# Group norm and attention on one core: the block sums moved into the accumulator's PSUM bank, the side work of the bursts reordered, the last two blocks inverted on VectorE

## Chip, cores and metric

One core of one Trainium2 chip. The metric is the time of one execution in device microseconds. Engines are named as in the profile: PE (TensorE matmul), PEld (weight load), DVE (VectorE), ACT (ScalarE), POOL (GpSimd), SP (the queue that issues DMA).

## The reference

```python
# x: (4, 512, 48, 48) fp32, so T = 2304 tokens per image, 8 heads of 64 channels
hn  = group_norm(x, 32 groups)
qkv = qkv_w @ hn + qkv_b                      # to fp16
w   = softmax((q * s).T @ (k * s))            # per image and head, 2304 x 2304
a   = w @ v                                   # fp32
out = x + proj_w @ a + proj_b
```

## The kernel before

The 16 pairs of heads (4 per image) are worked through in blocks of 512 queries (the last of each pair has 256). A block is 6 **bursts** (3 for the short one). A burst is three tiles of scores on PE, three exponentials on ACT, and the values of the burst before. There are 432 bursts, 108 per image ("batch"). Beside them runs a **list** of other PE work, cut into pieces: q, k and v chains of the coming pairs, and the output projection of the image before. A rule (`fill`) hands out pieces burst by burst.

The softmax's denominators: DVE adds the bursts' exponentials of a block into one tile (`acc`), and PE then sums that tile over its partitions with a matrix of ones (`sl`). PSUM has eight banks: three score tiles of two banks each, one bank for the accumulated values (`av`), one for all list chains (`pw`).

Names in the profile: `ps` are scores, `p` exponentials, `avx` and `slx` the copies of `av` and `sl` out of PSUM, `pqk` and `pv` the chains of q, k and v, `pr` the projection, `r` a residual tile (input and then output of a projection chain), `att` an attention result and `a` its conversion for the projection, `gmean` the group means of the next image's norm.

```python
    def values(u):
        ...
        if k == 0:
            av[0] = ps_av.tile([P, QB], F32, tag="av", ...)      # the only such bank
        ...                                                      # 6 or 12 matmuls
        if last:
            nc.vector.tensor_copy(avx[g, j][:, :n], av[0][:, :n])

    def add(u):
        ...
        nc.vector.tensor_tensor(acc[g, j], before, pt, ALU.add)

    def add_up(g, j):
        sl = chain_bank(f"sl_{g}_{j}")                           # the list's bank
        ...                                                      # matmuls: ones16 x acc
        nc.vector.tensor_copy(sx[:, :n], sl[:, :n])
        ...                                                      # the rows go out by DMA

    for n in range(len(stream) + 4):                             # one turn per burst
        scores(stream[n])
        values(stream[n - 1])
        add(stream[n - 1])
        if ended(n - 3):
            divide(*stream[n - 3][:2])      # inverses: to DRAM, back as rows, times avx
        if ended(n - 2):
            add_up(*stream[n - 2][:2])      # sums, and no list work in this burst
        else:
            fill(n, ended(n - 1))           # list work; closes the open chain at a block's end
    # cut: tails and conditions
```

A chain is four pieces of 4 matmuls (q, k, v), or one piece of 8 (projection).

## Time and profile before

| | before |
|---|---|
| median | 1800.25 us (4 runs, 1797.93 to 1801.34) |
| span of the profiled run | 1796.6 us |
| start to the first score | 120.5 us |
| batches of 108 bursts, by the starts of their first scores | 413.1, 435.5, 433.2 us |
| last batch, to the first score of its last burst | 353.3 us |
| from there to the end (tail) | 41.0 us |

The batch rows are read from the start times of the score matmuls. The lines of the profile stand in the prediction.

### The profile page before, as it was taken

To read this page: it belongs to the slowest core of one execution; us is meant where nothing else is said; L and a number is where in the kernel's file an instruction comes from. 1 tells how busy PE (TensorE), PEld (TensorE's weight loads), DVE (VectorE), ACT (ScalarE), POOL (GpSimd) and SP (SyncE) were. 2 spreads that over 40 slices of the span, in tenths; PEclk is the share of its full clock that TensorE was granted. 3 is DMA by queue.
4 is the path that set the end of the run, shared out by engine and by line. 5 is a ranking of instruction groups with operands and counts; after the bars stand their busy time and mean duration, and the time that the engine had idled before them with its cause. 6 is when DMAs were issued, how large, how long until landed. Compare 5 with 4: busy or idle time off the path is not lost. (4 is left out here: it accounts for less than half of the span.)

```text
span 1796.6 us, 26704 instructions
## 1 busy us (share of the span) xinstructions
PE 1652.7 (92%) x10706; PEld 649.1 (36%) x10706; DVE 1030.8 (57%) x1194; ACT 1220.1 (68%) x1297; POOL 334.7 (19%) x561
## 2 busy tenths in 40 slices
PE   4999997999999989899999998989999999999885
PEld 1333332333333343433333344343333334334443
DVE  5226557656555555756455555675555566666663
ACT  0027776677787775866677777685667888887971
POOL 1000122111121123210011113231011111222331
PEclk9999999999999999999999999999999999999998
DMA  5001022000000043310000014330000001104233
GB/s 194 0 1 31 19 50 78 10 13 13 10 14 16 17 112 118 90 39 13 10 13 16 13 40 122 107 92 13 13 10 13 14 15 23 53 16 132 61 107 110
DMA packets 90406, 82.15 MB, mean 46 GB/s; under 512 B 51488, under 2 KB 58144, under 8 KB 90272
## 3 DMA queue, kind: packets, MB, share of 16 engines
q1 hardware_dynamic: 83712, 62.75, 12.9%
q0 software_dynamic: 4592, 14.18, 2.7%
q10 hardware_dynamic: 1968, 3.41, 0.6%
q8 instruction: 86, 1.41, 0.3%
q14 instruction: 48, 0.39, 0.1%
HBM read 60.83 MB, written 19.17 MB: 45 GB/s over the span
## 5 line engine op out<-in xcount | busy, mean ns | idle before, releaser
L803 ACT ACTIVATE p<-ps 128x1024 f16<-128x1024 f32 x1296 | 1218.8, 1038 | 523.6 <-PE ps L796 523.4
L655 PE MATMUL pqk<-x,wqkv 128*64 128x512 f32 (+1 forms) x2560 | 530.4, 551 | 6.4 <-DVE x L628 4.4
L853 DVE TENSOR_TENSOR acc<-acc,p 128x3072 f16<-128x3072 f16 x272 | 482.3, 1773 | 31.0 <-ACT p L803 29.5
L796 PE MATMUL ps<-q,k 64*128 64x512 f16 (+1 forms) x2880 | 388.2, 360 | 64.0 <-ACT p L803 63.1
L820 PE MATMUL av<-p,v 128*64 128x512 f16 (+1 forms) x2880 | 363.7, 366 | 0.6 <-DVE avx L829 0.6
L655 PEld LDWEIGHTS pqk<-x,wqkv 128*64 128x64 f32 x2560 | 179.4, 137 | 255.3 <-issue 196.7
L796 PEld LDWEIGHTS <-k 64*128 64x128 f16 x2880 | 119.3, 94 | 412.3 <-issue 366.9
L696 PE MATMUL pv<-wqkv,x 128*64 128x512 f32 x1152 | 260.7, 599 | 4.3 <-DVE x L628 4.3
L885 POOL TENSOR_SCALAR in<-sums 128x8 f32<-128x8 f32 (+1 forms) x160 | 55.1, 345 | 964.3 <-DMA sums<-slx 957.9
L820 PEld LDWEIGHTS <-v 128*64 128x64 f16 x2880 | 125.6, 109 | 188.9 <-issue 149.6
L898 POOL TENSOR_TENSOR att<-avx,ib 128x512 f16<-128x512 f32 (+1 forms) x70 | 105.6, 1508 | 303.4 <-DMA ib<-row 275.9
L853 DVE TENSOR_TENSOR acc<-p,p 128x3072 f16<-128x3072 f16 x80 | 145.1, 1814 | 24.8 <-ACT p L803 24.7
L735 PE MATMUL pr<-a,whi 128*128 128x512 f32 (+1 forms) x320 | 126.1, 401 | 19.2 <-DVE r L743 10.3
L706 DVE TENSOR_TENSOR v<-pv,bv 128x256 f16<-128x256 f32 x144 | 54.4, 420 | 144.1 <-PE pv L696 144.0
L696 PEld LDWEIGHTS pv<-wqkv,x 128*64 128x64 f32 x1152 | 81.3, 138 | 148.2 <-issue 131.3
L664 DVE TENSOR_SCALAR k<-pqk,bqkv 128x512 f16<-128x512 f32 (+1 forms) x80 | 55.7, 696 | 109.4 <-PE pqk L655 109.4
L735 PE MATMUL pr<-a,wlo 128*128 128x512 f32 (+1 forms) x320 | 117.6, 374 | 0.0
L664 DVE TENSOR_SCALAR q<-pqk,bqkv 128x512 f16<-128x512 f32 (+1 forms) x80 | 55.6, 696 | 105.1 <-PE pqk L655 105.1
L829 DVE COPY avx<-av 128x512 f32<-128x512 f32 (+1 forms) x80 | 51.0, 637 | 92.9 <-PE av L820 92.0
L872 DVE COPY slx<-sl 128x512 f32<-128x512 f32 (+1 forms) x80 | 51.0, 637 | 86.2 <-PE sl L864 85.9
L743 DVE SCALAR_TENSOR_TENSOR r<-pr,bproj,r 128x512 f32<-128x512 f32 (+1 forms) x80 | 55.4, 693 | 47.6 <-PE pr L735 37.8
L735 PEld LDWEIGHTS pr<-a,whi 128*128 128x128 f32 x320 | 60.1, 188 | 59.1 <-issue 19.5
(48 smaller groups left out, 456.3 us busy)
## 6 DMA issues: line engine op xcount, KB each, us to landing
r<-x_dram SPq DMA_DIRECT2D x64, 256.0 KB, 2.9
ib<-row SPq DMA_DIRECT2D x128, 128.0 KB, 3.1
out_dram<-r SPq DMA_DIRECT2D x64, 256.0 KB, 3.0
x<-x_dram POOLq DMA_DIRECT2D x48, 256.0 KB, 3.3
x<-x_dram ACTq DMA_DIRECT2D x8, 256.0 KB, 7.0
x<-x_dram SPq DMA_DIRECT2D x8, 256.0 KB, 7.0
wqkv<-qkv_wT_dram SPq DMA_DIRECT2D x2, 1024.0 KB, 8.2
sums<-slx SPq DMA_DIRECT2D x128, 2.0 KB, 2.0
```

Source lines behind the costliest of these rows:

```text
L655: nc.tensor.matmul(pw[0][lo : lo + D, :n], wqkv[:, c, w0 + lo : w0 + lo + D], hn[b, c, j], start=(c == 0), stop=(c == NC - 1),)
L664: nc.vector.tensor_scalar(qk[g][part][:, o : o + n], pw[0][:, :n], bqkv[:, col : col + 1], SCALE, ALU.add, ALU.mult,)
L696: nc.tensor.matmul(pw[0][lo : lo + D, :], hn[b, c, i * P // QB][:, at + lo : at + lo + D], wqkv[:, c, 2 * C :], start=(c == 0), stop=(c == ...
L706: nc.vector.tensor_tensor(vv[b][half][:, i, :], pw[0][:, cols], bv[:, cols], ALU.add)
L735: nc.tensor.matmul(ps[:, :n], w[:, c, bass.ts(m, P)], at32[b, j][:, c, :n], start=(c == 0 and i == 0), stop=(c == NC - 1 and i == 1),)
L743: nc.vector.scalar_tensor_tensor(xt, ps[:, :n], bproj[:, m : m + 1], xt, ALU.add, ALU.add)
L796: nc.tensor.matmul(ps[:, h, a * n : (a + 1) * n], kt[rows, bass.ts(i, P)], qt[rows, o : o + n], start=True, stop=True,)
L803: nc.scalar.activation(pt[:, r], ps, AF.Exp)
L820: nc.tensor.matmul(av[0][lo : lo + D, :n], vv[b][pr // 2][:, i, pr % 2 * P + lo : pr % 2 * P + lo + D], pts[u][:, r, h, a * n : (a + 1) * ...
L853: nc.vector.tensor_tensor(acc[g, j], before, pt, ALU.add)
L885: nc.gpsimd.tensor_scalar(t[:, :, :per], sm, limit, None, op)
L898: nc.gpsimd.tensor_tensor(atts[g][:, o : o + n], avx.pop((g, j))[:, :n], ib[:, :n], ALU.mult)
```

## The change

Its intent: let every burst have list work, and let the sums no longer hold up the list's bank; convert attention results earlier than their projection needs them; spare the last two blocks the trip through DRAM. The core of the diff:

```diff
     def add_up(g, j):
-        sl = chain_bank(f"sl_{g}_{j}")
+        sl = ps_av.tile([P, QB], F32, tag="av", name=f"sl_{g}_{j}")
@@ the main loop
     for n in range(end):
+        if ended(n - 2):
+            add_up(*stream[n - 2][:2])          # ahead of the scores
         wanted(stream[n][0], n)
         scores(stream[n])
         values(stream[n - 1]); add(stream[n - 1])
-        if ended(n - 3): divide(...)
-        if ended(n - 2): add_up(...)
-        else: fill(n, ended(n - 1))
+        if ended(n - 3): check_sums(...); invert(...)      # unless inverted directly
+        if ended(n - 4): divide(...)
+        fill(n, 2.6 if ended(n - 1) else 0.0)    # in every burst
@@ fill
-        share = total[b] * (place + 1) / (per_batch - 2)
+        share = max(total[b] * (place + 1) / (per_batch - 1), done[b] + least)
         while beside[b]:
             if after > place or n < issued[0] + gap or (first and ended):
                 break                            # "first and ended": one chain's end per burst
@@ the last two blocks of the last pair
+        if direct(g, j):
+            nc.vector.reciprocal(inv[:, :n], source[:, :n])
+            nc.vector.tensor_tensor(atts[g][:, o : o + n], avx..., inv[:, :n], ALU.mult)
# cut: last add of those two blocks left to PE; order of the list (conversions ahead of other
# chains, statistics spaced by `gap` bursts); input loads from POOL's queue to SP's
```

More of the change, by code (lines that the diff above doesn't have):

```diff
@@ L630, in norm, with piece @@
             )
-    def piece(us, run, first=False, last=False):
-        return [us, run, first, last, 0, NG]
+    def piece(us, run, first=False, last=False, gap=0):
+        return [us, run, first, last, 0, NG, gap]
     qk = {}
@@ L721, in residual, with att32 @@
         res[b, j, m] = xt
-    def att32(b, j):
+    def att32(b, j, pairs=range(NC)):
         o, n = QBLOCKS[j]
-        t = work.tile([P, NC, QB], F32R, tag="a32", bufs=1, name=f"a32_{b}_{j}")
-        for c in range(NC):
-            nc.gpsimd.tensor_copy(t[:, c, :n], atts[b * NPAIR + c][:, o : o + n])
-        at32[b, j] = t
+        if (b, j) == (B - 1, NQ - 1):
+            if (b, j) not in at32:
+                t = ppool.tile([P, BURST, 2, QB], F16, tag="p", name="a32_last")
+                t = t.rearrange("p r h n -> p (r h n)")[:, : 2 * NC * n]
+                at32[b, j] = t.bitcast(F32R).rearrange("p (c n) -> p c n", c=NC)
+        else:
+            at32[b, j] = work.tile(
+                [P, NC, QB], F32R, tag="a32", bufs=1, name=f"a32_{b}_{j}"
+            )
+        for c in pairs:
+            engine = nc.vector if direct(b * NPAIR + c, j) else nc.gpsimd
+            engine.tensor_copy(
+                at32[b, j][:, c, :n], atts[b * NPAIR + c][:, o : o + n]
+            )
     def proj_chain(b, j, m):
@@ L746, in proj_chain, with proj_pieces @@
         nc.sync.dma_start(out[b, bass.ts(m, P), o : o + n], xt)
-    def proj_block(b, j):
-        pieces = []
+    def proj_pieces(b, j):
         def ahead(k):
-            if k < NQ * NC:
-                pieces.append(piece(0.0, lambda: residual(b, k // NC, k % NC)))
-        if j == 0:
-            ahead(0)
-            ahead(1)
-        pieces.append(piece(0.0, lambda: att32(b, j)))
-        for m in range(NC):
-            ahead(j * NC + m + 2)
-            pieces.append(
-                piece(
-                    QBLOCKS[j][1] / 290.0,
-                    lambda m=m: proj_chain(b, j, m),
-                    True,
-                    True,
-                )
-            )
-        return pieces
-    av, acc, pts, avx, sums = {}, {}, {}, {}, {}
+            return [
+                piece(0.0, lambda k=k: residual(b, k // NC, k % NC))
+                for k in range(k, min(k + 1, NQ * NC))
+            ]
+        convert = [piece(0.0, lambda: att32(b, j))]
+        chains = []
+        for m in range(NC):
+            pieces = ahead(0) + ahead(1) if (j, m) == (0, 0) else []
+            chain = piece(
+                QBLOCKS[j][1] / 290.0, lambda m=m: proj_chain(b, j, m), True, True
+            )
+            chains.append(pieces + ahead(j * NC + m + 2) + [chain])
+        return convert, chains
+    av, acc, pts, avx, sums, rowd = {}, {}, {}, {}, {}, {}
     stream = []
@@ L839, in new_att, with direct @@
             atts[g] = apool.tile([P, T], F16, tag="att", name=f"att_{g}")
+    def direct(g, j):
+        return g == NG - 1 and j >= NQ - 2
     def add(u):
-        g, j, k, _ = u
+        g, j, k, last = u
         pt = pts.pop(u)
         if k == 0:
-            acc[g, j] = pt
+            acc[g, j] = [pt]
             return
-        before = acc[g, j]
+        if last and direct(g, j):
+            acc[g, j].append(pt)
+            return
+        before = acc[g, j][0]
         if k == 1:
-            acc[g, j] = work.tile(
-                [P, BURST, 2, QB], F16, tag="acc", bufs=1, name=f"acc_{g}_{j}"
-            )
-        nc.vector.tensor_tensor(acc[g, j], before, pt, ALU.add)
+            acc[g, j] = [
+                work.tile(
+                    [P, BURST, 2, QB], F16, tag="acc", bufs=1, name=f"acc_{g}_{j}"
+                )
+            ]
+        nc.vector.tensor_tensor(acc[g, j][0], before, pt, ALU.add)
     def add_up(g, j):
@@ L857, in add_up @@
         per = QB // n
-        sl = chain_bank(f"sl_{g}_{j}")
-        t = acc.pop((g, j))
-        steps = [(r, a) for r in range(BURST) for a in range(per)]
-        for r, a in steps:
+        sl = ps_av.tile([P, QB], F32, tag="av", name=f"sl_{g}_{j}")
+        steps = [
+            (t, r, a)
+            for t in acc.pop((g, j))
+            for r in range(BURST)
+            for a in range(per)
+        ]
+        for i, (t, r, a) in enumerate(steps):
             for h in range(2):
@@ L867, in add_up @@
                     t[:, r, h, a * n : (a + 1) * n],
-                    start=((r, a) == steps[0]),
-                    stop=((r, a) == steps[-1]),
-                )
-        sx = work.tile([P, QB], F32, tag="rows", name=f"slx_{g}_{j}")
-        nc.vector.tensor_copy(sx[:, :n], sl[:, :n])
-        sums[g, j] = small.tile([P, 2, QB // P], F32, tag="sums", name=f"sums_{g}_{j}")
-        for h in range(2):
-            nc.sync.dma_start(sums[g, j][:, h, : n // P], sx[h * D : h * D + 1, :n])
-    def divide(g, j):
-        o, n = QBLOCKS[j]
-        per = n // P
-        sm = sums.pop((g, j))[:, :, :per]
-        ok = fine[:, :, :per]
+                    start=(i == 0),
@@ new lines, in add_up, with rows @@
+                    stop=(i == len(steps) - 1),
+                )
+        def rows():
+            sx = work.tile([P, QB], F32, tag="rows", name=f"slx_{g}_{j}")
+            nc.vector.tensor_copy(sx[:, :n], sl[:, :n])
+            sm = small.tile([P, 2, QB // P], F32, tag="sums", name=f"sums_{g}_{j}")
+            for h in range(2):
+                nc.sync.dma_start(sm[:, h, : n // P], sx[h * D : h * D + 1, :n])
+            sums[g, j] = sm
+            return sx
+        if direct(g, j):
+            source = rows() if n == QB else sl
+            inv = work.tile([P, QB], F32, tag="rows", name=f"inv_{g}_{j}")
+            nc.vector.reciprocal(inv[:, :n], source[:, :n])
+            nc.vector.tensor_tensor(
+                atts[g][:, o : o + n], avx.pop((g, j))[:, :n], inv[:, :n], ALU.mult
+            )
+            if source is sl:
+                rows()
+        else:
+            rows()
@@ L883, in divide, with check_sums @@
+    def check_sums(g, j):
+        n = QBLOCKS[j][1]
+        sm = sums[g, j][:, :, : n // P]
+        ok = fine[:, :, : n // P]
         for op, limit in ((ALU.is_ge, SUM_MIN), (ALU.is_le, SUM_MAX)):
             t = small.tile([P, 2, QB // P], F32, tag="in", name=f"in_{g}_{j}")
-            nc.gpsimd.tensor_scalar(t[:, :, :per], sm, limit, None, op)
-            nc.gpsimd.tensor_tensor(ok, ok, t[:, :, :per], ALU.mult)
+            t = t[:, :, : n // P]
+            nc.gpsimd.tensor_scalar(t, sm, limit, None, op)
+            nc.gpsimd.tensor_tensor(ok, ok, t, ALU.mult)
@@ L887, in divide, with invert @@
+    def invert(g, j):
+        n = QBLOCKS[j][1]
+        per = n // P
         inv = small.tile([P, 2, QB // P], F32, tag="inv", name=f"inv_{g}_{j}")
-        nc.vector.reciprocal(inv[:, :, :per], sm)
+        nc.vector.reciprocal(inv[:, :, :per], sums[g, j][:, :, :per])
         row = dram.tile([2, QB], F32, tag="row", name=f"row_{g}_{j}")
@@ L892, in divide @@
         )
+        rowd[g, j] = row
+    def divide(g, j):
+        o, n = QBLOCKS[j]
+        row = rowd.pop((g, j))
         ib = work.tile([P, QB], F32, tag="rows", name=f"ib_{g}_{j}")
@@ L908, in put, with put_run, put_qk, put_proj @@
         beside[b] += pieces
-    def put_qk(b, g, parts, after=0):
-        for part in parts:
-            for j in range(NQ):
-                put(b, qk_chain(g, part, j), after, g)
+    def put_run(b, run, *args, gap=0, us=0.0):
+        put(b, [piece(us, lambda: run(*args), us > 0, us > 0, gap)])
+    def put_qk(b, g, part, blocks=range(NQ), after=0):
+        for j in blocks:
+            put(b, qk_chain(g, part, j), after, g)
+    def put_proj(b, of, j, first=0, last=NC, after=0):
+        for pieces in projs[of, j][1][first:last]:
+            put(b, pieces, after)
+    def put_convert(b, of, j, after=0):
+        put(b, projs[of, j][0], after)
+    ends = [i for i, u in enumerate(stream) if u[3]][:NQ]
+    projs = {(b, j): proj_pieces(b, j) for b in range(B) for j in range(NQ)}
     for b in range(B):
         g = b * NPAIR
+        old = b - 1
         if b == 0:
@@ L919, in fast_path @@
                 if j < NC:
-                    put(b, [piece(0.0, lambda c=j: load_wproj(c))])
+                    put_run(b, load_wproj, j)
                 if j > 0:
-                    put(b, [piece(0.0, lambda c=j - 1: split_wproj(c))])
-                for part in (1, 0):
-                    put(b, qk_chain(g + 1, part, j), 0, g + 1)
-        else:
-            put_qk(b, g + 1, (0,))
-        put_qk(b, g + 2, (1, 0))
-        if b == B - 1:
-            put(b, proj_block(b - 1, 0))
-            put_qk(b, g + 3, (1, 0), per_pair - 1)
-            for j in range(1, NQ):
-                put(b, proj_block(b - 1, j))
-            for j in range(NQ):
-                end = 3 * per_pair + [i for i, u in enumerate(stream) if u[3]][j]
-                put(b, proj_block(b, j), end + 6)
+                    put_run(b, split_wproj, j - 1)
@@ new lines, in fast_path @@
+                put_qk(b, g + 1, 1, (j,))
+                put_qk(b, g + 1, 0, (j,))
+        else:
+            put_qk(b, g + 1, 0)
+        put_qk(b, g + 2, 1)
+        if b > 0:
+            put_convert(b, old, 0)
+        put_qk(b, g + 2, 0, (0, 1))
+        if b > 0:
+            put_proj(b, old, 0)
+            put_convert(b, old, 1)
+        put_qk(b, g + 2, 0, (2, 3))
+        if b == B - 1:
+            put_qk(b, g + 2, 0, (4,))
+            put_qk(b, g + 3, 1, after=per_pair - 1)
+            put_qk(b, g + 3, 0, (0,))
+            put_proj(b, old, 1)
+            for j in (2, 3, 4):
+                put_convert(b, old, j)
+                put_qk(b, g + 3, 0, (j - 1,))
+                put_proj(b, old, j)
+            put_qk(b, g + 3, 0, (4,))
+            for j in range(NQ - 1):
+                end = 3 * per_pair + ends[j] + (3 if j == NQ - 2 else 6)
+                put_convert(b, b, j, end)
+                put_proj(b, b, j, after=end + 1)
@@ L936, in fast_path @@
             continue
         if b > 0:
-            for j in range(3):
-                put(b, proj_block(b - 1, j))
+            put_proj(b, old, 1)
+            put_convert(b, old, 2)
+        put_qk(b, g + 2, 0, (4,))
         for j in range(NQ):
-            for part in (1, 0):
-                put(b, qk_chain(g + 3, part, j), per_pair - 1, g + 3)
-            put(b, [piece(0.0, lambda b=b, j=j: load_x(b + 1, j, (nc.gpsimd,)))])
+            put_qk(b, g + 3, 1, (j,), per_pair - 1)
+            put_qk(b, g + 3, 0, (j,), per_pair - 1)
+            put_run(b, load_x, b + 1, j, (nc.sync,))
@@ L945, in fast_path @@
             if j > 1:
-                put(b, [piece(0.0, lambda b=b, j=j: stats(b + 1, j - 2))])
-        rest = [
-            [piece(0.0, lambda b=b: stats(b + 1, NQ - 2))],
-            [piece(0.0, lambda b=b: stats(b + 1, NQ - 1))],
-            [piece(0.05, lambda b=b: group_mean(b + 1), True, True)],
-            [piece(0.05, lambda b=b: group_var(b + 1), True, True)],
-        ]
-        if b > 0:
-            pieces = proj_block(b - 1, 3) + proj_block(b - 1, 4)
-            chains = [i for i, p in enumerate(pieces) if p[2]]
-            for i, r in zip(reversed(chains[1:8:2]), reversed(rest)):
-                pieces[i + 1 : i + 1] = r
-            put(b, pieces)
-        else:
-            for r in rest:
-                put(b, r)
@@ L962, in fast_path @@
-        put(b, [piece(0.0, lambda b=b: norm(b + 1, 0))])
+                put_run(b, stats, b + 1, j - 2)
+            if j == 2 and b > 0:
+                put_proj(b, old, 2)
+                put_convert(b, old, 3)
+        if b > 0:
+            put_proj(b, old, 3, 0, 2)
+        put_run(b, stats, b + 1, NQ - 2, gap=2 * (b == 0))
+        if b > 0:
+            put_proj(b, old, 3, 2, 4)
+            put_convert(b, old, 4)
+        put_run(b, stats, b + 1, NQ - 1, gap=b == 0)
+        if b > 0:
+            put_proj(b, old, 4, 0, 1)
@@ L963, in fast_path @@
+        put_run(b, group_mean, b + 1, gap=b == 0, us=0.05)
+        if b > 0:
+            put_proj(b, old, 4, 1, 2)
+        put_run(b, group_var, b + 1, us=0.05)
+        if b > 0:
+            put_proj(b, old, 4, 2, 3)
+        put_run(b, norm, b + 1, 0)
+        if b > 0:
+            put_proj(b, old, 4, 3, 4)
         for i in range(NT):
@@ L965, in fast_path @@
             if i % 4 == 0 and i // 4 + 1 < NQ:
-                j = i // 4 + 1
-                put(b, [piece(0.0, lambda b=b, j=j: norm(b + 1, j))])
-        put_qk(b, g + 4, (1, 0), 2 * per_pair)
-        put_qk(b, g + 5, (1,), 3 * per_pair)
+                put_run(b, norm, b + 1, i // 4 + 1)
+        put_qk(b, g + 4, 1, after=2 * per_pair)
+        put_qk(b, g + 4, 0, after=2 * per_pair)
+        put_qk(b, g + 5, 1, after=3 * per_pair)
     for j in range(NQ):
@@ L989, in fast_path, with issue, fill, wanted @@
     done = dict.fromkeys(range(B), 0.0)
-    open_chain = [False]
-    def issue(b):
-        us, run, first, last, _, _ = beside[b].pop(0)
+    issued = [0]
+    def issue(b, n):
+        us, run = beside[b].pop(0)[:2]
         run()
         done[b] += us
-        open_chain[0] = (open_chain[0] or first) and not last
-    def fill(n, close):
-        b, place = min(n // per_batch, B - 1), n
+        issued[0] = n
+    def fill(n, least=0.0):
+        b = min(n // per_batch, B - 1)
         place = n - b * per_batch
-        share = total[b] * (place + 1) / (per_batch - 2)
+        share = max(total[b] * (place + 1) / (per_batch - 1), done[b] + least)
         ended = False
         while beside[b]:
-            _, _, first, last, after, _ = beside[b][0]
-            if after > place or (first and ended):
+            us, _, first, last, after, _, gap = beside[b][0]
+            if after > place or n < issued[0] + gap or (first and ended):
                 break
-            if done[b] > share and not (close and open_chain[0]):
+            if done[b] >= share and us > 0:
                 break
-            issue(b)
+            issue(b, n)
             ended = ended or last
-    def wanted(g):
+    def wanted(g, n):
         for b in range(B):
             while any(p[5] <= g for p in beside[b]):
-                issue(b)
+                issue(b, n)
     ended = lambda n: 0 <= n < len(stream) and stream[n][3]
-    for n in range(len(stream) + 4):
-        if n < len(stream):
-            wanted(stream[n][0])
-            scores(stream[n])
-        else:
-            alone[0] = True
-        if 0 < n <= len(stream):
+    end = len(stream)
+    for n in range(end):
+        if ended(n - 2):
+            add_up(*stream[n - 2][:2])
+        wanted(stream[n][0], n)
+        scores(stream[n])
+        if n > 0:
             values(stream[n - 1])
@@ L1030, in fast_path @@
         if ended(n - 3):
-            divide(*stream[n - 3][:2])
-        if ended(n - 2):
-            add_up(*stream[n - 2][:2])
-        else:
-            fill(n, ended(n - 1))
-    while beside[B - 1]:
-        issue(B - 1)
+            check_sums(*stream[n - 3][:2])
+            if not direct(*stream[n - 3][:2]):
+                invert(*stream[n - 3][:2])
+        if ended(n - 4):
+            divide(*stream[n - 4][:2])
+        fill(n, 2.6 if ended(n - 1) else 0.0)
+    alone[0] = True
+    values(stream[-1])
+    add(stream[-1])
+    att32(B - 1, NQ - 1, range(NC - 1))
+    add_up(NG - 1, NQ - 1)
+    att32(B - 1, NQ - 1, (NC - 1,))
+    while beside[B - 1]:
+        issue(B - 1, end)
+    check_sums(NG - 1, NQ - 1)
+    for pieces in projs[B - 1, NQ - 1][1]:
+        for p in pieces:
+            p[1]()
     good = small.tile([P, 1], F32, tag="good", bufs=1, name="good")
```

## The prediction

> **What bounds the kernel now.** I read the page's first part, then the waits, then the order of time in one stretch, then the chain at the end.
>
> ```profile
> PE 1652.7 (92%) x10706; PEld 649.1 (36%) x10706; DVE 1030.8 (57%) x1194; ACT 1220.1 (68%) x1297; POOL 334.7 (19%) x561
> ...
> L803 ACT ACTIVATE p<-ps 128x1024 f16<-128x1024 f32 x1296 | 1218.8, 1038 | 523.6 <-PE ps L796 523.4
> ```
>
> PE is the limit on average, ACT is idle for 523 us waiting for scores. So any idle time of PE between the first and the last score is time of the kernel. The waits of PE say how much there is:
>
> ```profile
> PE ps L796 <- ACT p L803: 63.1, 140, 0.5
> PE gmean L596 <- DVE mv L594: 30.0, 4, 19.6
> PE pr L735 <- DVE r L743: 10.3, 10, 3.2
> PE pr L735 <- POOL a L727: 8.8, 7, 3.0
> ...
> PE sl L864 <- DVE acc L853: 1.0, 2, 0.8
> ```
>
> The largest is scores waiting for exponentials, in pieces of at most half a microsecond; 19.6 of the 30.0 us on the group means lie before the stream starts. The sums of a block (L864) wait for almost nothing. The stretch 604 to 618 us, PE only, shows where the first wait comes from:
>
> ```profile
> 604.95 0.82 PE L796 MATMUL ps<-q,k 64*128 64x512 f16 x6
> 605.70 0.84 PE L820 MATMUL av<-p,v 128*64 128x512 f16 x6
> 606.37 3.60 PE L655 MATMUL pqk<-x,wqkv 128*64 128x512 f32 x16
> 609.90 0.82 PE L796 MATMUL ps<-q,k 64*128 64x512 f16 x6
> 610.65 0.84 PE L820 MATMUL av<-p,v 128*64 128x512 f16 x6
> 611.32 0.81 PE L864 MATMUL sl<-acc,ones 128*64 128x512 f16 x6
> 612.07 0.64 PE L796 MATMUL ps<-q,k 64*128 64x512 f16 x4
> 613.24 0.39 PE L796 MATMUL ps<-q,k 64*128 64x512 f16 x2 [0.53 <-ACT p L803]
> ```
>
> One burst is scores, values and a piece of the list (here a q chain). By start times a burst with 16 list matmuls takes 609.90-604.95 = 4.95 us, so scores and values take 1.52 (with 3.43 of list). The burst with the sums (0.75) has no list work: 2.17 us, and then PE idles, because ACT needs about 0.92 us for each of a burst's three exponentials (nine without a gap, from 581.6 us):
>
> ```profile
> 581.60 8.40 ACT L803 ACTIVATE p<-ps 128x1024 f16<-128x1024 f32 x9 [1.24 <-PE ps L796]
> ```
>
> By start times of scores in the trace, a short burst after a long one lasts 2.91 us whatever its work, and later short ones 2.75. **There is no slack: a burst whose list work is under about 1.4 us loses the difference.**
>
> DVE at the end of a block, 582 to 588 us:
>
> ```profile
> 582.87 0.69 DVE L829 COPY avx<-av 128x512 f32<-128x512 f32 x1 [3.26 <-PE av L820]
> 583.48 1.75 DVE L853 TENSOR_TENSOR acc<-acc,p 128x3072 f16<-128x3072 f16 x1
> 585.15 0.74 DVE L664 TENSOR_SCALAR k<-pqk,bqkv 128x512 f16<-128x512 f32 x1
> 586.82 0.69 DVE L872 COPY slx<-sl 128x512 f32<-128x512 f32 x1 [0.93 <-PE sl L864]
> ```
>
> After the last values of a block come the copy of the accumulator and then the last add; the add ends 2.47 us after those values in nearly all 80 blocks (585.23 here). The sums need it. Today a list piece and then a whole burst (1.52) stand between, so it is hidden.
>
> The chain that ended last, from 1768 us:
>
> ```profile
> 1768.47 2.60 PE pr L735 x10
> 1771.10 0.76 DVE r L743
> 1771.88 4.30 DMA out_dram<-r
> 1776.68 2.85 DMA out_dram<-r
> 1779.98 2.26 DMA out_dram<-r
> 1782.26 2.04 DMA r<-x_dram
> ```
>
> From 1771.9 on it is neither PE nor the inversion but the three residual buffers: an output must land before the next residual is fetched.
>
> **What the Trainium skill says.** "PSUM — Partial Sum Buffer", section "PSUM bank collisions raise a hardware error": PSUM is guarded by bank and quadrant, not by address. So sums in the accumulator's only bank must wait for its copy, and the next block's values for the copy of the sums; today only the first copy guards it ("av" waits 0.6 us in all). "VectorE: DVE Perf Modes", section "First, the fixed hardware budget": a reciprocal is an iterative divide with a repeat count of 8. The trace agrees in size: 8 elements take 203 ns and 4 take 178, some 6 ns an element, where a copy of 512 takes 691 in all. "DMA: Bandwidth & Descriptors", section "Anatomy of one DMA — SWDGE (gpsimd) path": about 2 us fixed per transfer, most of it the receipt; here 2 KB of sums take 2.0 us to land on the other path, the same size.
>
> **The change part by part.** (1) Sums. They move from after the next burst's values to before its scores, into the accumulator's bank, and every burst gets list work. Gain: the sum burst is no longer without list work. Cost: only the list work of one burst now stands between the last values and the sums. They can start 2.47+0.38 (drain of the values)+0.05 = 2.90 us after the last values' issue, and list work starts 0.21 after it, so PE waits 2.69 minus that list work. The diff asks for at least 2.6 there, but it also stops when a chain has ended in that burst and the next would begin. If a chain has one piece left, the burst gets 0.85 us and the wait is 1.84.
>
> I followed both list rules through all 432 bursts, counting pieces only (the rule of before puts 16, 0, 16, 8 matmuls where the trace has them). The 79 block ends within the stream get: 33 at least 2.69; 3 get 2.56; 11 get 2.07 (a projection chain, 8 matmuls, by bursts of 3.59 us); 11 get 1.71; 16 get 0.85; 5 get 0.05 or none. The waits: 3x0.13 + 11x0.62 + 11x0.98 + 16x1.84 + 5x2.67 = about 61 us, against 7 by the same rule before.
>
> Short bursts: bursts without list work fall from 100 to 43, those with only 0.43 to 1.03 us of it rise from 54 to 91 (a fixed amount of list spread over more bursts, and the minimum at block ends takes from the burst after it). Each summed against the floor of 2.91 or 2.75: 102 us before, 87 after. By batches of 108 bursts, waits and short bursts together: 27 to 35, 22 to 26, 22 to 26, and 38 to 60 in the last, where list work per burst (134.7/108 = 1.25 us) is under what ACT needs. Sum: **+39 us**. The rule gives 404, 421, 421 and 348 us for the batches of before; the trace has 413, 436, 433 and 353, so it holds, and 40 us are waits outside it.
>
> (2) Next values wait for the copy of the sums: it ends 1.11 us after the last sum's issue, values would start 1.05 after it. With the semaphore about 0.1 us, in some 60 blocks that ACT doesn't hide: **+6**.
>
> (3) Those 40 us outside: group mean 6.2 in the first batch, projections waiting for att or for r 9 in the second and 5 in the third, first v chains 4 each. Converting ahead and spacing the statistics take away perhaps 25. But statistics (4x0.68) and normalisations (4x0.54) now fall in the burst just before the sums' copy in some eight blocks, and delay it by 1 to 3 us each, more for the first batch's variance: about +12. Net **-13**.
>
> (4) DVE gets the reciprocal later relative to the sums' landing, so its 93 us of waiting there shrink; DVE is 57% busy, worth nothing on PE but part of (3). Input loads move from POOL to SP's queue: hidden.
>
> (5) The end. Two round trips through DRAM (2.4, 2.4 and 2.9 us and issues) go, for reciprocals of 512 and 256 elements, estimated 3.3 and 1.8 us from the 6 ns, and a second set of sum matmuls. Projection of the block before last could start 1 us earlier, the last chain's missing att 2 us. But from 1771.9 the three residual buffers set the pace, at 7 to 8 us per three outputs, and are unchanged, as are the 11 us after the last result. **-2**.
>
> Sum: 1799+39+6-13-2 = 1829. I take off 9, since single waits overlap in part: **1820 us**.
>
> **Rivals.** (a) What the change intends: all sum bursts' losses (80x0.74 = 59 us), the waits on conversions and 8 us of the end go, little comes: 1799-59-20-8, about 1712 at best, 1770 if half of it holds. For it: the 63.1 us wait. Against: list work is fixed, so what one burst gets another lacks, and the add's 2.47 us are real. (b) The last batch alone loses, 22 us, the rest comes out even by better order: 1815. (c) DVE backs up behind in-order statistics, long reciprocals and copies on which the accumulator's bank now hangs: 1845 or more. DVE's 57% speaks against a general backlog.
>
> **Range and chances.** A 2% change is 36 us: faster means under 1763, which needs (a) nearly whole; slower means over 1835, which needs my sum plus a little. Eight in ten: 1780 to 1845. Faster 0.07, same 0.68, slower 0.25.
>
> **What would show it.** PE waiting for acc before the sums: 50 to 65 us in place of 1.0. PE's scores waiting for ACT: 63 falling only to 45 to 60, with more of it in the last batch. The last batch 10 to 25 us longer, the second and third within 8 of before. From the last score to the end within 4 us of before. Reciprocals of 128x512 near 3.3 us. If the wait on acc is under 20 us, my step on the chain stop is wrong and the time is near 1770.

## The result, and the profile after

The changed kernel takes **1839.55 us** (4 runs, 1838.86 to 1840.27), ratio 1.022 (1.0202 to 1.0238): slower. A ratio here is of runs of both kernels in the same rounds; it is not quite the ratio of the medians quoted, since the kernel before was timed anew in each round. The forecast was +20 us; measured are +39.

| us | before | after | difference |
|---|---|---|---|
| start to first score | 120.5 | 121.7 | +1.2 |
| batches 1, 2, 3 | 413.1, 435.5, 433.2 | 421.4, 441.4, 439.3 | +8.3, +5.9, +6.1 |
| last batch | 353.3 | 379.8 | +26.5 |
| tail | 41.0 | 33.6 | -7.4 |

The loss is in the stream (the time from the first score to the first score of the last burst), more than half of it in the last batch. In the whole stream PE was idle for 134.2 us, against 98.3 before, and its matmuls, nearly the same in number, kept it busy for 1547.5 us against 1536.9 (the profile's sums over 121.73 to 1803.5 us and over 120.48 to 1755.65 us). So about 11 of the 47 us are not waits but longer busy time. Most of it fits the clock: in the trace's clock records the granted clock is 0.5 in 8 pieces of the stream, 37.5 us together, before in 4, 20.5 us; half of the difference, 8.5 us, is an estimate of what that costs. Each of these pieces begins during, or less than 2 us after, a PE wait of 1.4 us or more, though most of the 30 such waits of the changed kernel are not followed by one.

PE's waits after (who waited for what, us in total, times, longest), to hold against those of before:

```profile
PE ps L804 <- ACT p L811: 55.4, 136, 1.1
PE sl L886 <- DVE acc L870: 51.2, 41, 2.5
PE gmean L596 <- DVE mv L594: 26.6, 4, 19.6
PE av L828 <- DVE slx L896: 13.3, 7, 2.4
```

L804 is the scores line (L796 before), L886 the sums (L864 before). The wait for ACT fell by only 8 us; the wait of the sums for the last add rose from 1.0 to 51.2 us. And the next block's values now wait for the copy of the sums, in the bank that both use. One block's end shows it, PE first, then DVE:

```profile
568.47 0.84 PE L828 MATMUL av<-p,v 128*64 128x512 f16 x6
569.14 1.02 PE L656 MATMUL pqk<-x,wqkv 128*64 128x512 f32 x4
571.83 0.84 PE L886 MATMUL sl<-acc,ones 128*64 128x512 f16 x6 [1.66 <-DVE acc L870]
572.60 0.82 PE L804 MATMUL ps<-q,k 64*128 64x512 f16 x6
```

```profile
569.42 0.69 DVE L837 COPY avx<-av 128x512 f32<-128x512 f32 x1 [3.26 <-PE av L828]
570.03 1.75 DVE L870 TENSOR_TENSOR acc<-acc,p 128x3072 f16<-128x3072 f16 x1
571.70 0.74 DVE L665 TENSOR_SCALAR q<-pqk,bqkv 128x512 f16<-128x512 f32 x1
572.71 0.69 DVE L896 COPY slx<-sl 128x512 f32<-128x512 f32 x1 [0.28 <-PE sl L886]
```

The values end at 569.3, the copy and the add take DVE until 571.8, and the sums start 0.05 us later. Between stands one piece of 4 list matmuls, since a chain ended with it: this is the case of "0.85 us of list work" in the prediction (wait by its count 1.84, here 1.66). Meanwhile ACT has run out of scores as well: its three exponentials from 568.15 end at 571.00 and its next one starts at 573.03.

### The profile page after: what moved, and what is told of

Its sections match the earlier page's. It is cut to its first block, busy times and chain, and to the rows that moved or that the text cites. A ratio compares the mean times of both kernels' runs of the same rounds, so it can differ in the third digit from the quotient of the medians.

```text
span 1837.1 us, 26716 instructions
## 1 busy us (share of the span) xinstructions
PE 1664.0 (91%) x10724; PEld 660.4 (36%) x10724; DVE 1030.5 (56%) x1196; ACT 1224.0 (67%) x1297; POOL 328.2 (18%) x497
## 4 chain that ended last, share of the span: by engine, by line
PE 70%; ACT 14%; DVE 9%; issue 4%; DMA 2%; POOL 0%; SPq 0%; DVEq 0%; ACTq 0%
PE pqk L656 23%; ACT p L811 14%; PE av L828 13%; PE pv L697 13%; PE ps L804 12%; PE pr L747 6%; DVE acc L870 4%; PE sl L886 3%; DVE st L589 1%; DMA x<-x_dram 1%; DVE slx L896 1%; DMA r<-x_dram 1%; DVE r L755 0%; DVE q L665 0%; DMA sums<-slx 0%
## 5 line engine op out<-in xcount | busy, mean ns | idle before, releaser
L656 PE MATMUL pqk<-x,wqkv 128*64 128x512 f32 (+1 forms) x2560 | 539.7, 552 | 6.3 <-DVE x L628 5.3
L804 PE MATMUL ps<-q,k 64*128 64x512 f16 (+1 forms) x2880 | 384.4, 361 | 56.0 <-ACT p L811 55.4
L828 PE MATMUL av<-p,v 128*64 128x512 f16 (+1 forms) x2880 | 367.0, 368 | 15.4 <-DVE slx L896 13.3
L923 POOL TENSOR_SCALAR in<-sums 128x8 f32<-128x8 f32 (+1 forms) x160 | 106.9, 668 | 935.1 <-DMA sums<-slx 928.8
L656 PEld LDWEIGHTS pqk<-x,wqkv 128*64 128x64 f32 x2560 | 184.6, 138 | 232.8 <-issue 170.8
L804 PEld LDWEIGHTS <-k 64*128 64x128 f16 x2880 | 116.5, 94 | 399.2 <-issue 355.6
L828 PEld LDWEIGHTS <-v 128*64 128x64 f16 x2880 | 134.5, 109 | 208.3 <-issue 169.9
L870 DVE TENSOR_TENSOR acc<-p,p 128x3072 f16<-128x3072 f16 x80 | 140.3, 1754 | 107.9 <-ACT p L811 107.6
L886 PE MATMUL sl<-acc,ones 128*64 128x512 f16 (+1 forms) x576 | 68.4, 356 | 51.8 <-DVE acc L870 51.2
```

What stands on the lines that cost most here:

```text
L656: nc.tensor.matmul(pw[0][lo : lo + D, :n], wqkv[:, c, w0 + lo : w0 + lo + D], hn[b, c, j], start=(c == 0), stop=(c == NC - 1),)
L804: nc.tensor.matmul(ps[:, h, a * n : (a + 1) * n], kt[rows, bass.ts(i, P)], qt[rows, o : o + n], start=True, stop=True,)
L828: nc.tensor.matmul(av[0][lo : lo + D, :n], vv[b][pr // 2][:, i, pr % 2 * P + lo : pr % 2 * P + lo + D], pts[u][:, r, h, a * n : (a + 1) * ...
L870: nc.vector.tensor_tensor(acc[g, j][0], before, pt, ALU.add)
L886: nc.tensor.matmul(sl[lo : lo + D, :n], ones16, t[:, r, h, a * n : (a + 1) * n], start=(i == 0), stop=(i == len(steps) - 1),)
L923: nc.gpsimd.tensor_scalar(t, sm, limit, None, op)
```

## The experiments

All edits are against the changed kernel unless said. Waits, stream and tail are those of one profiled run each; the times of one kernel's runs lie 1 to 8 us apart.

**1. Sums put back.** Only the first part undone, as one bundle: place, bank and list rule.

```diff
-        sl = ps_av.tile([P, QB], F32, tag="av", name=f"sl_{g}_{j}")
+        sl = chain_bank(f"sl_{g}_{j}")
@@ main loop
-        if ended(n - 2): add_up(...)                       # ahead of the scores
...
-        fill(n, 2.6 if ended(n - 1) else 0.0)
+        if ended(n - 2): add_up(...)
+        else: fill(n, ended(n - 1))                        # closes the open chain, as before
# cut: the list's share per burst as before
```

> The changed kernel with the first part alone undone: the sums of a block again in the list's bank, after the next burst's scores and values, with no list work in that burst; list order, early conversions and VectorE inversion stay. Theory A (the place of the sums costs the time): PE's wait for acc before the sums falls from 51 us to under 5, its wait for ACT rises to about 65, and the time is 1785 to 1805. Rival B (the new list order, with statistics and conversions at the block ends, costs it): 1825 or more.

1791.25 us, ratio to before 0.9924 (0.9903 to 0.9946). PE waits 3.3 us for acc before the sums and 66.8 for ACT. So the new handling of the sums is the loss, and the rest of the change is a small gain: against this kernel, the full change costs 1.022/0.9924 = 1.030, some 53 us (48 by medians, 49.3 in the streams of the profiled runs). Rival B falls. Which member of the bundle costs the time is for the next runs to say.

**2. The last add set aside.** Wrong (the sums lack a burst), yet within the tolerance of the comparison.

```diff
-        nc.vector.tensor_tensor(acc[g, j][0], before, pt, ALU.add)
+        out = pt if last else acc[g, j][0]
+        nc.vector.tensor_tensor(out, before, pt, ALU.add)
```

> Wrong on purpose: the last add of a block writes its burst's own tile, so VectorE does the same work but the sums don't wait for it (they lack one burst). Theory A says that the 51 us of PE waiting for acc are time of the kernel nearly in full: time 1780 to 1800, wait for acc under 5, wait for ACT within 10 of 55. Rival C (PE's wait only stands where PE would have waited for ACT anyhow, and short bursts set the time): the wait for ACT grows by 30 or more and the time stays above 1820.

1820.55 us, ratio 1.0088: neither forecast. The wait for acc is gone and the wait for ACT didn't grow, but only some 19 us are won. PE and then DVE at the same block end show why:

```profile
571.98 0.84 PE L887 MATMUL sl<-acc,ones 128*64 128x512 f16 x6
572.75 0.82 PE L804 MATMUL ps<-q,k 64*128 64x512 f16 x6
574.90 0.84 PE L828 MATMUL av<-p,v 128*64 128x512 f16 x6 [1.33 <-DVE slx L897]
```

```profile
571.84 1.75 DVE L871 TENSOR_TENSOR p<-acc,p 128x3072 f16<-128x3072 f16 x1
573.51 0.75 DVE L665 TENSOR_SCALAR q<-pqk,bqkv 128x512 f16<-128x512 f32 x1
574.17 0.68 DVE L897 COPY slx<-sl 128x512 f32<-128x512 f32 x1
```

The sums no longer wait, but their copy stands in DVE's queue behind the same add (and a copy of q), and the next values need the bank that the copy frees. PE's wait moved from the sums to the values: these waited 13.3 us and now wait 52.2, in 41 waits. The two together fell only from 64.5 us to 55.7 (3.5 of it sums that wait for the accumulator's copy). The Trainium skill, "PSUM — Partial Sum Buffer", section "Engine vs sequencer instructions", says that VectorE's queue is strict FIFO; this trace agrees, the copy starts at 574.17 although its sums had ended at 572.8.

**3. The last add dropped**, to part that queue from the bank. Wrong again.

```diff
+        if last:
+            return
         before = acc[g, j][0]
```

> Wrong on purpose: the last add of a block is left out, so VectorE has the copy of the accumulator and then at once the copy of the sums. In the run with the add set aside the wait only moved from the sums (51 us) to the next values (52 us, behind the same add in VectorE's queue). If that queue is the cause, both waits fall together to under 20 us and the time is 1775 to 1795. If the accumulator's single bank alone makes the wait (two copies in series without any add), values still wait 40 us or more and the time is above 1810.

1782.49 us, ratio 0.9897: as the queue's theory says. Values wait 16.9 us for the copy and the sums 3.9 for the accumulator's. Against the change (1.022/0.9897 = 1.033, some 57 us) this also counts the DVE time of the dropped adds and matmuls that were busy for 13 us less (1534.1 us in the stream; the clock was 0.5 for only 6.8 us of it), so it is not the wait alone; but two copies in series without the add are not what costs 40 us.

**4. The minimum held over the end of a chain.** The prediction named the stop at a chain's end as what breaks the 2.6 us minimum.

```diff
-            if after > place or n < issued[0] + gap or (first and ended):
+            if after > place or n < issued[0] + gap or (
+                first and ended and done[b] >= floor):      # floor = done[b] at entry + least
```

> The minimum of 2.6 us of list work at a block's end holds over the end of a chain (one condition). The list rule then leaves 5 of 61 us of waits for acc, but takes list work from the bursts after, whose shortfall grows from 87 to 125 us: theory A with this sum says 1815 to 1830. If the chain stop is the whole cause, 1785 to 1800. If a new chain right after the end of the last one waits for the single list bank instead, 1835 or more, with PE waiting for VectorE's copies out of that bank.

1931.03 us, ratio 1.0714. The worst of all, in the direction of the third forecast and far beyond. The list has a single bank, and a chain that ends at a block's end is copied out by DVE only after the accumulator's copy and the add. PE in this run:

```profile
621.05 1.02 PE L656 MATMUL pqk<-x,wqkv 128*64 128x512 f32 x4
624.40 4.49 PE L656 MATMUL pqk<-x,wqkv 128*64 128x512 f32 x12 [2.33 <-DVE k L665]
```

The chain stop that looked like the fault protects from this wait. PE waits 24.1, 20.8 and 9.9 us for the copies of k and q and 18.9 for r there, and 77.2 us for ACT; the wait for acc is down to 7.3, as the count said. The second line shows a further cost: the 12 matmuls after the wait take 4.49 us, where 16 take 3.60 in the prediction's stretch. At 624.6 us the granted clock goes to 0.5 for 3.4 us. It is at 0.5 for 85.3 us of this stream (37.5 in the changed kernel), and PE is busy for 1581.3 us (1547.5). So of the 94 us that the stream is longer, 61 are PE's idle time and some 34 longer busy time, of which the clock explains about 24 (an estimate: half of 85.3 less 37.5).

**5. No minimum at all.**

```diff
-        fill(n, 2.6 if ended(n - 1) else 0.0)
+        fill(n)
```

> The changed kernel without the minimum of 2.6 us at a block's end (one argument). The prediction's count says that the minimum only moves the loss: waits for acc 61 to 75 us, short bursts 87 to 74, time the same within 5 us of 1840. If the minimum does hide the add, the time rises by 15 us or more; if it is what starves the bursts after it, it falls by 10 or more.

1836.94 us, ratio 1.0193 (1.0172 to 1.0214): unchanged within the noise. Waits for acc rise from 51.2 to 62.0, waits for ACT fall from 55.4 to 44.8. The list's work is fixed: what the minimum gives a block's end, the next bursts lack. This agrees with the prediction's count (62 is in its 61 to 75, the time within 5 us of 1840).

**6. Sums between scores and values, in the list's bank**, list work in every burst, minimum 1.7, chains closed ahead of the sums.

```diff
         scores(stream[n])
+        if ended(n - 2):
+            add_up(*stream[n - 2][:2])                     # sl in chain_bank again
         values(stream[n - 1]); add(stream[n - 1])
...
-        fill(n, 2.6 if ended(n - 1) else 0.0)
+        fill(n, 1.7 if ended(n - 1) else 0.0, ended(n - 1))
```

> Sums in the list's bank, between a burst's scores and its values, and list work in every burst, minimum 1.7 us at a block's end, chains closed before the sums. ACT has a burst of scores to work on while PE waits for the add, and the copy of the sums lies beside the values. Theory A: 1785 to 1805, wait for acc 15 to 30 us, wait for ACT 45 to 65. Rival B: 1825 or more, as in the run with the sums put back.

1817.8 us, ratio 1.0083: between the two forecasts, a miss. The waits of the sums are now for the copies of q (11.5), k (10.1) and r (5.8 us): a chain closed just ahead of them is copied behind the add, as in experiment 4. The profile's waits there don't add up to the whole distance from the sums-put-back kernel, so this run shows the new wait and not its full account.

**7. VectorE inversion undone as well**, on the kernel of experiment 1.

```diff
     def direct(g, j):
-        return g == NG - 1 and j >= NQ - 2
+        return False
# and at the end: divide of the last block but one, sums, rest of the list, invert, divide, convert
```

> The kernel with the sums put back, and the last two blocks inverted by the trip through DRAM again. It parts the 11 to 14 us that the other parts gained: if the VectorE inversion of the last two blocks brings most of it, 1797 to 1803 and the tail after the last burst's scores 40 to 44 us; if list order and early conversions bring it, 1789 to 1794, since the residual buffers set the tail's pace (prediction's step 5: 2 us).

1797.54 us, ratio 0.998 (0.9965 to 0.9995). Its tail is 48.5 us, longer than before's 41.0, with 11.5 us of PE waiting for the last conversion, because the end had to be put together anew; so only its stream is used. That ends at 1749.4 us against 1755.6 in the kernel before. 1.3 us of this is an earlier start; the stream itself is 1630.3 us against 1635.2, so list order, spacing and early conversions bring 5 us, about as much as single runs differ. PE's idle time in the stream fell by only 2 us (98.3 to 96.4). Its waits for att conversions and for r fell from 8.8 + 10.3 to 2.1 + 6.3 there (the new one at the end apart), but its wait for ACT rose from 63.1 to 68.4:

```profile
PE ps L804 <- ACT p L811: 68.4, 156, 0.5
...
PE pr L747 <- DVE r L755: 6.3, 9, 1.5
...
PE pr L747 <- POOL a L738: 2.1, 2, 1.4
```

**8. Sums in the scores' banks.** Neither the list's bank nor the accumulator's.

```diff
-        sl = ps_av.tile([P, QB], F32, tag="av", name=f"sl_{g}_{j}")
+        sl = ps_s.tile([P, 2, QB], F32, tag="ps", name=f"sl_{g}_{j}")[:, 0, :]
@@ main loop: after scores, values and add of the next burst, and list work in that burst too
+        if ended(n - 2): add_up(...)
+        fill(n, 1.7 if ended(n - 1) else 0.0)
```

> Sums in one of the three score tiles' banks, after the next burst's scores and values, and list work in every burst, minimum 1.7 us: neither the list's bank nor the accumulator's is tied to VectorE's queue. Count by the list rule: 23 us less than the kernel before in the stream, waits for acc about 11; with the other parts' gain 1765 to 1780. Rival: the score tile taken from the rotation makes ACT or the scores wait, wait for ACT 90 us or more and 1800 or more.

1760.34 us, ratio 0.9769 (0.9748 to 0.979): faster than both, and under the 1765 to 1780 forecast. Waits for acc have left the first nine rows of PE's waits, the wait for ACT is 49.8 us. Batches 407.2, 420.5, 419.6 and 355.7.

**9. The same with chains of two pieces** (8 matmuls, 1.71 us) in place of four.

```diff
-            piece(n / 600.0, lambda c=c: one(c), c == 0, c == NC - 1)
-            for c in range(NC)
+            piece(n / 300.0, lambda c=c: (one(c), one(c + 1)), c == 0, c == NC - 2)
+            for c in range(0, NC, 2)
# the v chains likewise
```

> As the run with the sums in the score banks, and list chains cut in two pieces of 1.71 us in place of four of 0.85, so that hardly a burst has less than ACT's floor needs. List rule: short bursts 60 us in place of 102, 44 us less than before in the stream: 1740 to 1760. If the shortfall per burst is not what sets PE's wait for ACT, it stays at the time of the run with four pieces.

1740.85 us, ratio 0.9662 (0.9646 to 0.9678). PE's wait for ACT is 39.1 us. In the stretch from 562 to 580 us the bursts last 3.24 us each from score to score, and the one with the sums, which has list work too, 3.99:

```profile
566.58 0.84 PE L829 MATMUL av<-p,v 128*64 128x512 f16 x6
567.34 0.84 PE L887 MATMUL sl<-acc,ones 128*64 128x512 f16 x6
567.98 1.91 PE L656 MATMUL pqk<-x,wqkv 128*64 128x512 f32 x8
569.82 0.82 PE L805 MATMUL ps<-q,k 64*128 64x512 f16 x6
```

Here the floor that the prediction read from the trace (a burst under 2.91 us loses the rest) was used to choose the pieces, and the run agrees with it: batches 394.6, 414.3 and 413.6. The last batch got longer by 5, 360.5.

**10. Two pieces, but four in the last batch**, where list work is scarce.

```diff
+        s = 1 if g > (B - 1) * NPAIR else 2                # matmul groups per piece
```

> As the run with sums in the score banks and chains of two pieces, but the chains of the last batch, where a burst has only 1.25 us of list work on average, stay in four pieces. In that run the last batch took 360 us, with four pieces 356, in the kernel before 353. If coarse pieces starve the bursts between them there, the last batch falls by 4 to 8 us and the time is 1732 to 1739; if not, it stays at 1739 to 1745.

1738.09 us, ratio 0.9653 (0.9632 to 0.9675); last batch 355.8. The batch behaved as expected; the total differs from experiment 9 by less than the intervals. It has the lowest time, 3.5% under the kernel before.

## Why the prediction was wrong

The mechanism of the loss was right and the direction too; the sum came out at half the size, because a gain that it set against the loss hardly came. By its own steps:

- **The wait on the add (step 1).** Predicted: 50 to 65 us of PE waiting for acc where 1.0 stood. Measured 51.2. The wait for ACT was to be 45 to 60, and is 55.4. The changed kernel's trace has the block ends that the list rule gave: 16 with one piece of 4 matmuls (26.6 us of waits together, 29.4 predicted), 11 with 8 of a projection (6.9), 11 with 1.71 us of list work (8.6), none waiting among those with at least 2.56. Experiments 1, 3 and 5 confirm that this is the cost, and that the minimum only moves it. That a removal of the chain stop would help was implied by naming it as the fault; experiment 4 shows the opposite.
- **Sums' part as a whole.** The prediction has +39 (step 1), +6 (step 2) and, inside step 3, +12 for copies of the sums delayed by statistics. Together 57. Less the 9 taken off for overlap, 48. Undoing that part alone moves the time by 48 us by medians, 53 by ratios, 49.3 in the stream. That the sum fits is partly luck: of the 49.3 us only 38.7 are idle time of PE, and 10.6 are longer busy time (8.5 by the estimate from the lower clock), for which the prediction has no term. The last batch, forecast at 10 to 25 us longer, is 26.5 longer; batches two and three (within 8) are 5.9 and 6.1 longer.
- **The step that failed: "Converting ahead and spacing the statistics take away perhaps 25", in step 3.** Experiment 7 has this part without the other two: 5 us of stream and 2 us of PE's idle time are gone, not 25; with the VectorE inversion left in (experiment 1) the stream gains 2.7. The step counted waits as if each were time of the kernel. PE's waits for conversions and r did fall by about 11 us, and those for group means inside the stream from 10.4 (30.0 less 19.6) to only 8.9 (29.0 less 20.1). But PE's wait for ACT rose by 5, and some 4 us of new waits for copies by DVE came up. That a burst cut short by a removed wait meets ACT's floor instead would explain the 5 us; no run tests it apart. The gain of the first three batches (1.6, 6.5 and 0.7 us) is partly lost again in the last (3.8 longer).
- **Beside that step.** In the changed kernel itself these waits (group means, r, att, first v chains) fell from 28.4 us in the stream to 10.5, so what the step is worth depends on the waits beside it. The prediction's total of 28 for them is right, its reading of single ones loose: the first v chains wait 2.2 and 2.1 us, not 4 each, and projections wait 5.5 us in the second batch, not 9.
- **The tail (step 5).** Predicted -2, "within 4 us of before"; measured -7.4. The term was too small. The reciprocals are what was read from the small ones (3.3 and 1.8 estimated):

```profile
L907 DVE RECIPROCAL inv<-slx 128x512 f32<-128x512 f32 x1 | 3.4, 3352 | 0.1
L907 DVE RECIPROCAL inv<-sl 128x256 f32<-128x256 f32 x1 | 1.8, 1758 | 1.6 <-PE sl L886 1.6
```

What was wrong is that the residual buffers keep setting the pace. The chain that ended last, in the changed kernel:

```profile
1813.22 8.94 PE pr L747 x40
1822.18 0.76 DVE r L755
1822.96 0.33 SPq L758
1823.35 2.44 DMA r<-x_dram
```

PE runs 40 projection matmuls without a break before residuals matter again. With the sums put back but the inversion kept, the tail is 39.3 us (experiment 1), so the inversion alone does not bring it. Experiment 8, whose sums stand as late as before but whose every burst has list work, has a tail of 34.9: it is list work in every burst that goes with the shorter tail, and not the earlier place of the sums. How that acts on the residual loads was not traced.

By the profiled runs the account closes. Measured are +49.3 us for the sums' part (changed kernel against experiment 1), -2.7 for the rest in the stream (experiment 1 against before), +1.2 at the start and -7.4 in the tail, together 40; the prediction had +48, -25, 0 and -2 for them. The second term makes the miss, and the tail made it smaller.

One slip in the prediction's sums changes little: scores and values are 1.52 us there, but 1.52 + 0.75 is 2.27, not the 2.17 that it reads for the burst with the sums.

Rival (a) of the prediction, that every burst's list work gains what was intended, is not false in itself: experiment 8 (1760 us) passes the half of it (1770) once the sums stand where neither the accumulator's bank nor DVE's queue is waited for. Experiments 9 and 10 needed coarser pieces too.

## What to carry to other kernels

Before moving an instruction earlier, list what its inputs' producer still has in its in-order queue: the time that lay between was cover, and a shared bank adds a second wait behind the same queue. When a pipeline has a floor per step, count work per step, not on average: pieces should be about as large as the shortfall, and a removed wait may be worth only what remains above the floor (experiment 7 fits this, but doesn't test it apart). Look at the busy time of the same matmuls too, and not only at waits: here the kernels with more long waits of PE also ran them slower (1581.3 us in experiment 4, 1536.9 before). When a fix moves a wait from one consumer to another, look for the common queue.

## What the Trainium skill lacked or had wrong

- "VectorE: DVE Perf Modes" names the reciprocal's repeat count of 8 but no time for it. Here 512 elements per partition take 3352 ns and 256 take 1758 (one instruction each): 6.2 ns an element, against 691 ns for the multiply of 512.
- "PSUM — Partial Sum Buffer" tells how to guard a bank, not that a bank shared by two accumulations ties PE to everything ahead of the copy in VectorE's queue: of 64.5 us of waits of sums and next values, 55.7 remained when only the data dependence was removed.
- No page that I read tells what it costs to take a tile out of a rotation of three score tiles for one step: in experiment 8 no such cost was visible, PE's wait for ACT fell from 63.1 to 49.8 us; list work in every burst, which came with it, may hide one.
